# An attention and window-convolution kernel: x channels spread over 128 partitions, three of every four used

## The chip, the cores and the metric

The kernel runs on one core of one Trainium2 chip. The metric is the device time of one execution in microseconds; the time before is the median of three runs, 3556.07 us (3543.9 to 3556.36).

## The reference

One image of 48 channels and 256 x 256 pixels goes through two layers, each with a group normalisation ahead of it and a residual around it.

```python
# layer 0: x (1, 48, 256, 256), 16 groups of 3 channels in _gn
qkv = einsum('bchw,oc->bohw', _gn(x), w_qkv)        # 144 channels
q, k, v = split(dwconv3x3(qkv, w_dw), 3)            # depthwise 3x3
q, k, v = heads(unfold(.))                          # 4x4 patches, 8 heads, 96 x 4356
attn = softmax(_l2norm(q)^T _l2norm(k) * temperature)
x = x + einsum('bchw,oc->bohw', fold(v attn^T), w_proj)
# layer 1: windows of 64 x 64
x = x + sum_t einsum('bcphqw,wW,hH,cC->bCpHqW', windows(_gn(x)), Ws[t], Hs[t], Cs[t])
```

The patches of the outer border are all zero; they count only in the softmax's sum.

## The kernel before

All is float32. Channels lie on partitions. Image tensors with 48 channels are held as two halves: upper image rows (or the upper of two parts of a tile) on partitions 16 to 63, lower ones on 64 to 111; partitions 0 to 15 are cleared (`OFF = 16`, `PF = 112`, `rows_of`). `begin` moves one such tensor with two transfers of 48 rows, one for each half, in turn on the queues it is given.

The work goes through these stages.

1. **Head.** x is loaded into `xr` in ten parts (`parts`, most of 16 image rows of each half) over the queues of SyncE and ScalarE, while ScalarE clears the first 16 partitions (`clear`, L120). VectorE takes statistics of each two image rows as a part is there (`bn_stats`, L451), then `group_stats` makes mean and 1/deviation of each group with two products with `gm`. They are folded into the weights: `wq` (two heads) and `wr` (six heads), both held twice, for the two halves, and into `bias`. `gm`, `wq`, `wr` and `wp` (the projection) are zeroed by VectorE and filled by small loads on the GpSimd queue (L98 to L114), `wq` and `wr` copied from half to half by a transfer (L112).
2. **First convolution.** The product with `wq` for two heads (L512), out of `xr`, with ScalarE and VectorE in turn adding the bias into `oi` (L521, L523), and stores to the DRAM tensor `t1[0]`, 36 channels in transfers of 32 and 4 (L528), half of them on SyncE, half on GpSimd.
3. **Depthwise convolution of head 0** (`depthwise_first`), whose outcome goes to DRAM (`qkv`) in patch order.
4. **Attention**, head by head in an order written out by hand: `scores` (L370, L638), `weigh` (L672), and between them the depthwise convolution of the next head, and, in head 0, the product for the other six heads strip by strip (`Strip`, `xs`, L203). In the last head the first three x tiles of the projection (`xt`) and most of the first patch tile (`pot0`, in `kt` buffers) are loaded on SyncE.
5. **Projection** (`project`, L837), eight tiles in `order`: the product with `wp` over patches (`pot`, loaded on SyncE from `os_`, L907), the residual added in place by VectorE (L844), statistics (L846), and a store to the DRAM tensor `x1s` on GpSimd. x tiles from the fourth on (`pxt`, `pieces`) are loaded on SyncE and ScalarE. `pieces` (`lxq`) stays and is the first band of the last layer.
6. **Last layer**: over channels (L1008, weights `csn`, which also carry the mean through a partition that holds ones), over w (L1032), over h (L1051), the residual (L1065), the output on GpSimd (L1069). Loads of the next rows and pieces are issued one at a time on SyncE (`begin_load`), each behind a tiny transfer (`turns`) that waits for work just done; `load_piece` is one transfer of 48 rows and four image rows.

Stages 1, 2 and 5 are put in order by the framework's scheduler within each engine, except TensorE's order in parts of 5; stages 4 and 6 are in the order as written. A hardware transfer of SyncE or ScalarE uses one of eight semaphores in turn, and so waits for the one eight before it.

Of the kernel before, what the change touches and what calls it, by code (L numbers as in the profile page):

```python
# [21 lines left out]
OFF = 16  # L22
PF = OFF + P2
# [26 lines left out]
def conv_preact_kernel(  # L50
# [44 lines left out]
    rows_of = [slice(OFF + s * C, OFF + (s + 1) * C) for s in range(2)]  # L95
    gm = const.tile([PF, PF], F32, name="gm")
    nc.vector.memset(gm, 0.0)
    nc.gpsimd.dma_start(out=gm[OFF:, OFF:], in_=gmat)  # L98
    wq = const.tile([PF, 64], F32, name="wq")
    nc.vector.memset(wq, 0.0)  # L100
    wr = const.tile([PF, M1], F32, name="wr")
    nc.vector.memset(wr, 0.0)
    wp = const.tile([PF, PF], F32, name="wp")
    nc.vector.memset(wp, 0.0)
    for h in range(NH):
        o = h * HC if h < H0 else (h - H0) * HC
        nc.gpsimd.dma_start(
            out=(wq if h < H0 else wr)[rows_of[0], o : o + HC].rearrange("c (z e) -> c z e", z=3),
            in_=w_qkvT.rearrange("c (z h e) -> h c z e", z=3, h=NH)[h],
        )  # L110
    for w in (wq, wr):
        nc.gpsimd.dma_start(out=w[rows_of[1]], in_=w[rows_of[0]])  # L112
    for r in rows_of:
        nc.gpsimd.dma_start(out=wp[r, r], in_=w_projT)  # L114

    def clear(t, n=OFF, value=0):

        _, a, b = t.shape
        to = plain[:n, value : value + 1].rearrange("p (u v) -> p u v", u=1).to_broadcast([n, a, b])
        nc.scalar.copy(t[:n], to)  # L120
# [7 lines left out]
    taps = ExitStack()  # L128
    diag = taps.enter_context(tc.tile_pool(name="diag", bufs=1)).tile([NP1, 9, NP1], F32, name="diag")
# [43 lines left out]
    def begin(to, rows, engs, into=True):  # L173

        for s in range(2):
            a, b = (to[rows_of[s]], rows[s])
            engs[s % len(engs)].dma_start(out=a if into else b, in_=b if into else a)
# [9 lines left out]
    class Strip:  # L187
# [5 lines left out]
        def load(self):  # L193
            self.xs = xss[self.j % len(xss)]
            begin(self.xs, both_halves(xc, SR * self.j, SR), (nc.sync,))

        def run(self, pool):
            self.ot = ots[self.j % len(ots)]
            for i in range(0, SR, 2):
                ps = pool.tile([128, 2, 512], F32, name="big")  # L200
                for s in range(2):
                    r = slice(s * 64, min(PF, s * 64 + 64))
                    nc.tensor.matmul(  # L203
                        ps[:M1, s, :],
                        lhsT=wr[r],
                        rhs=self.xs[r, i : i + 2, :].rearrange("p a b -> p (a b)"),
                        start=True,
                        stop=True,
                    )
# [223 lines left out]
    with tc.tile_pool(name="xn", bufs=1) as xnp, tc.tile_pool(name="cst", bufs=1) as cst, tc.tile_pool(  # L433
# [10 lines left out]
        parts = [16] * 7 + [8, 4, 4]  # L444
        st0 = cst.tile([PF, HALF * W // 512, 6], F32, name="st0")
        for i, LR in enumerate(parts):
            j = sum(parts[:i])
            begin(xr[:, j : j + LR, :], both_halves(xc, j, LR), (nc.sync, nc.scalar))
            clear(xr[:, j : j + LR, :])
            for i in range(0, LR, 2):  # L450
                nc.vector.bn_stats(st0[:, (j + i) // 2, :], xr[:, j + i : j + i + 2, :].rearrange("p a b -> p (a b)"))  # L451
        group_stats(st0, mean0, rstd0, cst, nps)
        for g, w in enumerate((wq, wr)):
            nc.vector.tensor_scalar_mul(w, w, rstd0)
            m = w.shape[1]
            pb = nps.tile([128, 1], F32, name="pb0", tag="pstat")
            if g:
                nc.tensor.matmul(pb[:m], lhsT=w[:64], rhs=mean0[:64], start=True, stop=True)
# [45 lines left out]
        for n in range(QR // OR):  # L504
            ot = ois[n % len(ois)]
            for i in range(0, OR, 2):
                ps = pw.tile([128, 2, 512], F32, name="pw")
                for c in range(2):
                    for s in range(2):
                        r = slice(s * 64, min(PF, s * 64 + 64))  # L510
# [13 lines left out]
            for c in range(2):  # L524
                to = t1[0][:, 1 : H + 1, :].rearrange("c (s y) x -> c s y x", s=2)
                to = to[:, :, c * QR + n * OR : c * QR + (n + 1) * OR, :]
                for a, b in ((0, 32), (32, M0)):
                    (nc.gpsimd if c else nc.sync).dma_start(out=to[a:b], in_=ot[c * 64 + a : c * 64 + b])  # L528
# [10 lines left out]
    xss = [cv.tile([PF, SR, W], F32, name=f"xs{i}") for i in range(2)]  # L539

    def edges():
# [4 lines left out]
        for t in xss:  # L546
            nc.gpsimd.memset(t[:OFF], 0.0)

# [39 lines left out]
    with tc.tile_pool(name="ahead", bufs=2) as ah, tc.tile_pool(name="ae", bufs=3) as ae, tc.tile_pool(  # L588
# [113 lines left out]
        def load_pot0(ki, half, c0, c1, eng):  # L702
# [3 lines left out]
            r = OFF + half * C  # L706
# [14 lines left out]
        with tc.manual_schedule():  # L721
# [3 lines left out]
            for h in range(NH):  # L725
                more = h + 1 < NH
                rows = {r: Depthwise(h + 1, r) for r in range(CR + 1)} if more else {}
                for g in range(NG):
                    p, d, n = rows.get(g - 2), rows.get(g - 1), rows.get(g)

                    if not more and g == 0:
# [4 lines left out]
                        for t in xts:  # L736
                            nc.gpsimd.memset(t[:OFF], 0.0)
                        pot0 = [ah.tile([128, 2, 512], F32R, name="kt", bufs=14) for _ in range(KS)]
                        pot0 = [t.bitcast(F32).rearrange("p a (b n) -> p (a b) n", b=2) for t in pot0]
                        for t in pot0:  # L740
                            nc.gpsimd.memset(t[:OFF], 0.0)
# [87 lines left out]
        def project(k, pot, part, xt, new):  # L829
# [4 lines left out]
            for ki in range(KS):  # L834
                ps = new(PY)
                for y in range(0, PY, 2):
# [3 lines left out]
                        rhs=pot(ki)[:PF, :, (part * PY + y) * PX : (part * PY + y + 2) * PX],  # L840
# [9 lines left out]
        def in_big(n):  # L850

            ps = big.tile([128, 2, 512], F32, name="big")
            return ps[:PF].rearrange("p a (b x) -> p (a b) x", x=W)
# [21 lines left out]
    def load_piece(yw, i, s, y, n, eng):  # L875

        y0 = yw * WS + s * HW + i * PR + y
        eng.dma_start(out=piece(yw, i)[rows_of[s], y : y + n, :], in_=x1s[:, y0 : y0 + n, :])

    with tc.tile_pool(name="pjx", bufs=1) as pjx, tc.tile_pool(name="pj", bufs=1) as pj, tc.tile_pool(name="pjs", bufs=1) as pjs, tc.tile_pool(  # L880
# [4 lines left out]
        pots = [pj.tile([PF, KK, NP], F32, name=f"pot{t}") for t in range(3)]  # L885
        for t in pots + pxts:
            clear(t)
        clear(pieces.rearrange("p a y x -> p (a y) x"), 64 + CF, 1)
        csn = l1c.tile([64 + CF, T3 * C], F32, name="csn")
        nc.gpsimd.memset(csn, 0.0)  # L890
        for r in rows_of:
            nc.scalar.dma_start(out=csn[r].rearrange("c (t d) -> c t d", t=T3), in_=Cs.rearrange("t c d -> c t d"))
        at = pjs.tile([PF, PF + 1], F32, name="at")
        nc.gpsimd.memset(at, 0.0)
        for o in (0, PF):
            nc.gpsimd.memset(at[:, o : o + 1], 1.0)

        def both_pieces(i):

            return pieces[:PF, i : i + 2].rearrange("p a y x -> p (a y) x")  # L900

        xus = [[xts[1]], [xts[2]], [pxts[0]], [pxts[1]], [pieces[:PF, NPC], pxts[2]], [both_pieces(2)]]
        xus.append([pieces[:PF, 0], pieces[:PF, 1]])
        for k, xus_k in enumerate(xus, 1):
            yw, i = order[k]
            ot = pots[k % 3]
            nc.sync.dma_start(out=ot[OFF:], in_=ov[yw * 2 + i])  # L907
# [22 lines left out]
        with tc.manual_schedule(engines={mybir.EngineType.PE}):  # L930
# [5 lines left out]
            mcol = pjs.tile([PF, PF + 1], F32, name="mcol")  # L936
            nc.vector.tensor_scalar_mul(mcol, at, mean1)
            occupy(nmx)
            nc.vector.tensor_scalar_mul(csn[:PF], csn[:PF], rstd1)
# [202 lines left out]
```

## Time and profile before

| | |
|---|---|
| median of three runs | 3556.07 us |
| profiled execution, its own time | 3557.27 us |
| its span, first to last instruction | 3555.5 us |
| mean granted TensorE clock | 0.979 |
| TensorE matmul busy | 3314.1 us (93%) |
| VectorE busy | 1958.1 us (55%) |
| ScalarE busy | 1952.7 us (55%) |
| GpSimd busy | 589.7 us (17%) |
| moved by DMA | 380.20 MB, mean 107 GB/s |

A busy share is an average over stages that differ. The page's 40 slices of 89 us show the busy tenths of each engine, the tenths of the 16 DMA engines and the GB/s that they moved. The view by stage gives for a window the busy time of each engine with the number of its instructions, the granted clock, the DMA share and GB/s. The waits name who waited for whom, with the total, the number and the longest. The chain of waits follows the work that ended last back from step to step.

### The profile page before, as it was taken

How to read it: one execution, taken by the hardware profiler on the slowest of the kernel's cores; microseconds unless marked ns; L12 is line 12 of the kernel's file. 1: busy time of each engine (PE TensorE's matmuls, PEld its weight loads, DVE VectorE, ACT ScalarE, POOL GpSimd, SP SyncE). 2: the span in 40 equal slices, each digit the busy share in tenths (PEclk: the TensorE clock that was granted, in tenths of full speed). 3: DMA queues.
4: the chain of work that ended last, by engine and by line, in shares of the span. 5: the costliest groups of instructions: out<-in, count | busy, mean ns of one | idle time of the engine just before them, and what ended most of it. 6: DMA issues, size and time to landing. Idle time of an engine off the chain costs nothing.

```text
span 3555.5 us, 63466 instructions
## 1 busy us (share of the span) xinstructions
PE 3314.1 (93%) x25964; PEld 1852.0 (52%) x25964; DVE 1958.1 (55%) x2965; ACT 1952.7 (55%) x2891; POOL 589.7 (17%) x660
## 2 busy tenths in 40 slices
PE   0596999999999999999999999999999999996898
PEld 0243455555555555555555555555555555542576
DVE  5272666138834882588258825882687222226544
ACT  3234676657755765566556655765576444442243
POOL 2221111012211221122012201220122020000123
PEclk9898999999999999999999999999999999997999
DMA  8546666543332333233333333333233322119764
GB/s 146 139 126 156 162 167 159 165 139 95 87 87 76 93 87 86 79 95 85 83 91 96 81 86 86 95 80 88 83 93 88 79 65 49 30 38 257 205 165 113
DMA packets 232498, 380.20 MB, mean 107 GB/s; under 512 B 77794, under 2 KB 176482, under 8 KB 229128
## 3 DMA queue, kind: packets, MB, share of 16 engines
q1 hardware_dynamic: 191094, 252.76, 26.1%
q0 software_dynamic: 36544, 110.12, 13.9%
q10 hardware_dynamic: 4562, 13.19, 1.9%
q8 instruction: 207, 3.39, 0.4%
q14 instruction: 91, 0.75, 0.1%
HBM read 230.82 MB, written 144.90 MB: 106 GB/s over the span
## 4 chain that ended last, share of the span: by engine, by line
PE 86%; DMA 5%; DVE 2%; SPq 1%; ACT 1%; issue 1%; ACTq 0%; POOL 0%; POOLq 0%; DVEq 0%
PE big L370 39%; PE big L672 36%; PE pb L1032 2%; PE pa L1008 2%; DMA xs<-in_x_dram 2%; PE pc L1051 2%; DMA pot<-os__70 2%; PE big L203 2%; PE dps L247 1%; DVE acc L258 1%; PE pst L615 1%; SPq L344 0%; DVE st L846 0%; DMA kt<-qkv 0%; DMA pad<-t 0%
## 5 line engine op out<-in xcount | busy, mean ns | idle before, releaser
L638 ACT ACTIVATE e<-big,nmx 128x1024 f32<-128x1024 f32 x1024 | 1144.1, 1117 | 899.8 <-PE big L370 887.3
L370 PE MATMUL big<-kt,qt 128*128 128x512 f32 x6144 | 1458.2, 395 | 26.8 <-DMA kt<-qkv 24.5
L672 PE MATMUL big<-e,vn 128*32 128x512 f32 x12288 | 1348.5, 593 | 1.0 <-DVE vn L656 1.0
L370 PEld LDWEIGHTS big<-kt,qt 128*128 128x128 f32 x6144 | 1142.4, 189 | 367.1 <-issue 120.2
L686 DVE TENSOR_TENSOR oacc<-big,oacc 128x1024 f32<-128x1024 f32 x359 | 438.4, 1221 | 768.2 <-PE big L672 768.2
L672 PEld LDWEIGHTS big<-e,vn 128*32 128x32 f32 x12288 | 384.5, 110 | 881.9 <-issue 815.8
L258 DVE SCALAR_TENSOR_TENSOR acc<-pad,dwt,acc 126x1024 f32<-126x1024 f32 x592 | 765.5, 1293 | 34.4 <-ACT acc L239 18.7
L328 POOL DMA_DIRECT2D qkv<-o x72 | 52.8, 734 | 1336.6 <-ACT o L312 1336.6
L322 POOL TENSOR_TENSOR ol<-o,oh 126x1024 fp32r<-126x1024 f32 x78 | 185.2, 2374 | 273.2 <-DVE ss L273 198.0
L652 DVE TENSOR_REDUCE zt<-zs 128x1 f32<-128x5 f32 x256 | 38.6, 151 | 325.1 <-ACT e L638 288.6
L638 ACT ACTIVATION_READ_ACCUMULATOR e<-big,nmx 128x1 f32 x1024 | 195.9, 191 | 0.0
L312 ACT COPY o<-acc 126x1024 f32<-126x1024 f32 x74 | 161.5, 2183 | 0.0
L239 ACT ACTIVATE acc<-pad,dwt 126x1024 f32<-126x1024 f32 x74 | 84.1, 1136 | 86.0 <-DMA pad<-t 76.7
L210 ACT ACTIVATE ot<-big,bias 108x1024 f32<-108x1024 f32 x64 | 68.1, 1111 | 113.4 <-PE big L203 76.1
L1039 ACT COPY lyt<-pb 128x1024 f32<-128x1024 f32 x69 | 69.8, 1012 | 107.0 <-PE pb L1032 107.0
L697 POOL DMA_DIRECT2D os__70<-oacc x86 | 50.3, 593 | 424.1 <-DVE oacc L686 414.3
L247 PE MATMUL dps<-pad,diag 126*126 126x512 f32 x216 | 96.5, 607 | 22.9 <-DMA pad<-t 22.9
L269 ACT ACTIVATE sq<-acc 126x1024 f32<-126x1024 f32 x74 | 78.2, 1057 | 59.6 <-DVE acc L258 48.5
L344 POOL DMA_DIRECT2D kt<-qkv x44 | 22.9, 542 | 518.8 <-PE big L370 507.7
L273 DVE TENSOR_REDUCE ss<-sq 126x64 f32<-126x1024 f32 x80 | 97.3, 1218 | 6.5 <-ACT sq L269 6.5
L1018 DVE COPY lzt<-pa 128x864 f32<-128x864 f32 (+1 forms) x69 | 67.3, 998 | 59.6 <-PE pa L1008 59.6
L837 PE MATMUL pps<-pot,wp 112*112 112x512 f32 x112 | 60.9, 699 | 39.5 <-DVE pxt L844 22.6
(154 smaller groups left out, 1944.3 us busy)
## 6 DMA issues: line engine op xcount, KB each, us to landing
pad<-t SPq DMA_DIRECT2D x238, 254.0 KB
t<-ot SPq DMA_DIRECT2D x64, 435.4 KB
qkv<-ol POOLq DMA_DIRECT2D x78, 336.0 KB, 6.5
qkv<-oh POOLq DMA_DIRECT2D x70, 336.0 KB, 5.9
qt<-qkv SPq DMA_DIRECT2D x176, 96.0 KB
xs<-in_x_dram SPq DMA_DIRECT2D x64, 192.0 KB
out_dram<-lrt POOLq DMA_DIRECT2D x96, 128.0 KB, 3.6
qkv<-o POOLq DMA_DIRECT2D x72, 168.0 KB, 3.5
```

The costliest lines, as they stand in the source:

```text
L203: nc.tensor.matmul(ps[:M1, s, :], lhsT=wr[r], rhs=self.xs[r, i : i + 2, :].rearrange("p a b -> p (a b)"), start=True, stop=True,)
L239: nc.scalar.mul(self.acc, self.pad[:, 0:KS, 0:W], dwt[:, self.h, 0:1])
L247: nc.tensor.matmul(ps[:, i, :], lhsT=diag[:, tap, :], rhs=self.pad[:, y : y + 2, dx : dx + W], start=(tap == 0), stop=(tap == 8),)
L258: nc.vector.scalar_tensor_tensor(self.acc, self.pad[:, dy : dy + KS, dx : dx + W], dwt[:, self.h, tap : tap + 1], self.acc, ALU.mult, ALU.add,
L269: nc.scalar.activation(self.sq, self.acc, AF.Square)
L273: nc.vector.tensor_reduce(self.ss, self.sq.rearrange("p a (x b) -> p x a b", b=KS), AX.XY, ALU.add)
L312: nc.scalar.copy(self.o.rearrange("p (a b) x -> p a b x", a=KS), self.acc.rearrange("p a (x b) -> p a b x", b=KS))
L322: eng.tensor_sub(self.ol, self.o, self.oh.bitcast(F32))
L370: nc.tensor.matmul(ps[:, i, :], lhsT=qt[:, r, q0 : q0 + 128], rhs=kts[2 * j + i][:, r // 2, :], start=(r == 0), stop=(r == 2),)
L638: nc.scalar.activation(e[:, j * 1024 : (j + 1) * 1024], ps.rearrange("p a b -> p (a b)"), AF.Exp, bias=nmx[:, b : b + 1], accum_out=zs[:, ...
L672: nc.tensor.matmul(ps[p * 32 : (p + 1) * 32, u, :], lhsT=vn[:, c * 32 : (c + 1) * 32], rhs=e[:, n * 512 : (n + 1) * 512], start=(i == 0), ...
L686: nc.vector.tensor_add(oaccs[h, pair], ps, old)
```

## The change

The halves now lie on partitions 0 to 63 and 64 to 127, and in each group of four partitions three hold channels and the fourth a fill (`SP3 = 4`, `PF = 128`). `begin` and `load_piece` move a half with three transfers of 16 rows at steps of four partitions (every third channel each). The fill is written to all 128 partitions of the tile ahead of the load, with 0 in the head and 1 from the projection on, so that the fourth partitions serve as the ones of the last layer.

Weights come into this layout on the chip: each is loaded once, densely, with 48 channels on 48 partitions, and TensorE multiplies it with a matrix of ones and zeros (`spread`, `one_half`, `twice`). `xs` and `wr` keep 48 dense partitions a half, at 0 and 64; the statistics are brought there by products with `fold`. `pot` has 96 dense partitions from 0 on, and `wp` maps these to the 128. x is loaded in eight parts of other sizes, and the statistics are written after all loads in the program. The stores of the first convolution are one transfer of 36 rows instead of 32 and 4.

```diff
-OFF = 16
-PF = OFF + P2
+SP3 = 4
+PF = 128
-    rows_of = [slice(OFF + s * C, OFF + (s + 1) * C) for s in range(2)]
+    rows_of = [[slice(s * 64 + k, (s + 1) * 64, SP3) for k in range(3)] for s in range(2)]
-    nc.gpsimd.dma_start(out=gm[OFF:, OFF:], in_=gmat)
-    for h in range(NH):
-        o = h * HC if h < H0 else (h - H0) * HC
-        nc.gpsimd.dma_start(out=(wq if h < H0 else wr)[rows_of[0], o : o + HC]...)
-    for w in (wq, wr):
-        nc.gpsimd.dma_start(out=w[rows_of[1]], in_=w[rows_of[0]])
-    for r in rows_of:
-        nc.gpsimd.dma_start(out=wp[r, r], in_=w_projT)
-    def clear(t, n=OFF, value=0):
...
+        nc.gpsimd.dma_start(out=w48, in_=w_qkvT)
+        nc.gpsimd.dma_start(out=g48, in_=gmat[0:C, 0:C])
+        nc.gpsimd.dma_start(out=p48, in_=w_projT)
...
+        ps = through(spread, w48)
+        nc.vector.tensor_copy(mixed(wq, H0), by_head(ps, 0, H0))
+        ps = through(twice, w48)
+        nc.vector.tensor_copy(mixed(wr, NH - H0), by_head(ps, H0, NH))
+        nc.vector.tensor_copy(fold, through(one_half[:, 0], twice))
+        nc.vector.tensor_copy(gs, through(g48, spread))
+        nc.vector.tensor_copy(gm, through(spread, gs))
...
+        nc.vector.tensor_copy(wp, through(wt[:, 0], one_half[:, 0], [(wt[:, 1], one_half[:, 1])]))
+    def fill(t, eng, value=0.0):
+        if eng is nc.scalar:
+            _, a, b = t.shape
+            src = plain[:, int(value) : int(value) + 1].rearrange("p (u v) -> p u v", u=1)
+            eng.copy(t, src.to_broadcast([128, a, b]))
+        else:
+            eng.memset(t, value)
     def begin(to, rows, engs, into=True):
-        for s in range(2):
-            a, b = (to[rows_of[s]], rows[s])
-            engs[s % len(engs)].dma_start(out=a if into else b, in_=b if into else a)
+        for k in range(3):
+            for s in range(2):
+                a, b = (to[rows_of[s][k]], rows[s][k::3])
+                engs[s % len(engs)].dma_start(out=a if into else b, in_=b if into else a)
...
-            begin(self.xs, both_halves(xc, SR * self.j, SR), (nc.sync,))
+            for s, rows in enumerate(both_halves(xc, SR * self.j, SR)):
+                nc.sync.dma_start(out=self.xs[s * 64 : s * 64 + C], in_=rows)
...
-        parts = [16] * 7 + [8, 4, 4]
+        parts = [8, 24, 32, 32, 16, 8, 4, 4]
         for i, LR in enumerate(parts):
             j = sum(parts[:i])
+            fill(xr[:, j : j + LR, :], nc.vector if i in (0, 2) else nc.scalar)
             begin(xr[:, j : j + LR, :], both_halves(xc, j, LR), (nc.sync, nc.scalar))
-            clear(xr[:, j : j + LR, :])
-            for i in range(0, LR, 2):
+        for j in range(0, HALF, 16):
+            for i in range(0, 16, 2):
                 nc.vector.bn_stats(...)
...
+                nc.tensor.matmul(pf[:, 0:1], lhsT=fold, rhs=mean0, start=True, stop=True)
+                nc.tensor.matmul(pf[:, 1:2], lhsT=fold, rhs=rstd0, start=True, stop=True)
...
-                for a, b in ((0, 32), (32, M0)):
-                    (nc.gpsimd if c else nc.sync).dma_start(out=to[a:b], in_=ot[c * 64 + a : c * 64 + b])
+                (nc.gpsimd if c else nc.sync).dma_start(out=to, in_=ot[c * 64 : c * 64 + M0])
...
                         for t in xts:
-                            nc.gpsimd.memset(t[:OFF], 0.0)
+                            nc.gpsimd.memset(t, 1.0)
-                        for t in pot0:
-                            nc.gpsimd.memset(t[:OFF], 0.0)
...
-        eng.dma_start(out=piece(yw, i)[rows_of[s], y : y + n, :], in_=x1s[:, y0 : y0 + n, :])
+        for k in range(3):
+            eng.dma_start(out=piece(yw, i)[rows_of[s][k], y : y + n, :], in_=x1s[k::3, y0 : y0 + n, :])
...
-        for t in pots + pxts:
-            clear(t)
-        clear(pieces.rearrange("p a y x -> p (a y) x"), 64 + CF, 1)
+        pots = [pj.tile([P2, KK, NP], F32, name=f"pot{t}") for t in range(3)]
+        fill(pxts[0], nc.scalar, 1.0)
+        fill(pxts[1], nc.scalar, 1.0)
+        fill(pieces.rearrange("p a y x -> p (a y) x"), nc.scalar, 1.0)
+        fill(pxts[2], nc.scalar, 1.0)
+        nc.scalar.dma_start(out=c48.rearrange("c (t d) -> c t d", t=T3), in_=Cs.rearrange("t c d -> c t d"))
+        nc.tensor.matmul(pcs, lhsT=spread, rhs=c48, start=True, stop=True)
+        nc.vector.tensor_copy(csn, pcs)
...
-            nc.sync.dma_start(out=ot[OFF:], in_=ov[yw * 2 + i])
+            nc.sync.dma_start(out=ot, in_=ov[yw * 2 + i])
```

## The prediction

> **What bounds the kernel now.** I read the page's 40 slices first, then the table by stage (busy time of each engine in chosen windows), then the chain of waits, and for the two stages that the change touches the waits and the timeline.
>
> The slices and the page's chain:
>
> ```profile
> PE   0596999999999999999999999999999999996898
> DMA  8546666543332333233333333333233322119764
> GB/s 146 139 126 156 162 167 159 165 139 95 87 87 76 93 87 86 79 95 85 83 91 96 81 86 86 95 80 88 83 93 88 79 65 49 30 38 257 205 165 113
> ...
> PE 86%; DMA 5%; DVE 2%; SPq 1%; ACT 1%; issue 1%; ACTq 0%; POOL 0%; POOLq 0%; DVEq 0%
> ```
>
> TensorE is full for some 30 slices in the middle (the attention, 753 to 3160 us). Nothing of the change lies on that path. It is idle at the start and thins out near the end, exactly where the DMA row is high. So the change is worth what it does at the two ends. The stages there:
>
> ```profile
> 14.00:24.00 10.00, 0.00 (x0) 0.00 (x0) 6.58 (x22) 3.47 (x2) 1.14 (x2) 1.00 1.02 161
> 24.00:34.00 10.00, 0.00 (x0) 0.00 (x0) 4.95 (x9) 3.38 (x1) 1.20 (x3) 1.00 1.06 173
> ...
> 110.00:116.00 6.00, 5.84 (x56) 2.03 (x48) 3.74 (x3) 2.39 (x3) 3.32 (x6) 1.00 0.92 234
> ...
> 3230.00:3256.00 26.00, 4.59 (x11) 1.59 (x9) 5.97 (x10) 0.00 (x0) 1.02 (x2) 0.63 1.02 265
> 3256.00:3285.00 29.00, 21.73 (x37) 8.19 (x38) 28.07 (x40) 1.28 (x1) 4.10 (x8) 0.79 1.02 243
> 3285.00:3302.00 17.00, 10.97 (x18) 3.81 (x17) 7.46 (x10) 0.00 (x0) 1.02 (x2) 0.80 1.00 311
> ```
>
> The columns are window, length, busy us of PE, PEld, DVE, ACT, POOL, the clock, the DMA share and GB/s. While x is loaded (0.7 to 75 us) the 16 DMA engines are busy all the time, yet move only 160 to 173 GB/s. In the projection (3197 to 3302) they are full too, at 243 to 311. The stores of the first convolution reach 234 GB/s with 0.92 of the engines. So a full DMA queue can go faster than it does on x.
>
> Who waits for it, at the start and in the projection (from the waits and the chain):
>
> ```profile
> DVE st L451 <- DMA xr<-in_x_dram: 29.2, 5, 12.1
> ...
> L451 DVE BATCH_NORM_STATS2 st<-xr 112x6 f32<-112x512 f32 x64 | 38.6, 676 | 30.5 <-DMA xr<-in_x_dram 29.2 <-issue 1.3
> ...
> 3229.47 26.14 DMA pot<-os__70
> ...
> 3268.26 32.87 DMA pot<-os__70
> ```
>
> VectorE's statistics are 38.6 us of work drawn out to 84.4 us. In the projection two stretches of 26 and 33 us are waits for loads (the chain names pot; VectorE was waiting for the x piece, which landed behind it).
>
> **The change, part by part.**
>
> *Loading x (head).* The group's data must land before statistics can end. Work on the parts is released by their landing at 13.65, 23.52, 33.42, 42.64 and 51.78 us, 9.5 us per 16 rows (1.57 MB, both halves), 165 GB/s; all 12.58 MB take 73.5 us. Each transfer of 48 rows becomes three of 16 rows.
>
> The trace has no such transfer. The nearest row is the store of the first convolution, 234 GB/s, which would give 53.8 us. [...] I take 57.5 us.
>
> [...] x's channels lie 256 KiB apart, before and after. If that holds x at 165 GB/s, nothing is gained. The stores at 234 GB/s have a pitch that is no power of two, so the trace doesn't exclude it. This is a rival below.
>
> *Fills.* A load now waits for a fill of its rows on all 128 partitions; before, 16 rows were cleared beside the load. VectorE: `row` 1x1134 took 1.00 us, 0.88 ns an element, so 1.8 us (8 image rows) and 7.2 us (32). ScalarE: 128x10240 took 8.72 us, so 5.2 us for 24 rows, 7.0 for 32, 3.6 for 16. In the program's order the first fill stands eleventh on VectorE, at about 1.9 us: the first transfers start at 3.8 us instead of 0.7, the second part at 7.7 (table load to 2.5, then 5.2 us); the first part's 0.79 MB cover 3.6 us of that. Later fills (14 us of ScalarE) stand behind at most eight transfers in flight, 1.9 MB or more of a queue's own, some 17 us. Cost: 3 us, in the sum. If the cover were gone, 7 us more.
>
> *Weights through products.* Three loads replace thirteen (`gm`, `wq`, `wr`, `wp`) on POOL's queue. The old ones crawled behind x (`wr` landed after 37.6 us); the new ones are issued by about 4 us, when x has hardly begun. Eight products and about 12 small VectorE copies (0.15 to 0.3 us each, 0.5 us for a product as in `pm`) now stand ahead of the statistics on VectorE: it ends fills at about 11.5 us and this chain at about 20 us. The first 32 image rows land at 19.4, so it costs about 1 us. If `p48` landed as late as `wr` did, statistics would start at 40 us and end at 79.
>
> *Statistics.* 64 x 0.604 us. Landing at 0.45 us per image row from 5 us on: parts at 20.4 (32 rows), 34.8, 49.2, 56.4, 60, 62, 63.5. VectorE: 20.5 to 30.2, 34.8 to 44.5, 49.2 to 58.9, then in one run to 63.7, 66.1, 67.3, 68.5. Before: 84.4. **Head: -16 us.** Behind it two `fold` products stand on TensorE before the second convolution product: +1 us.
>
> *First convolution.* One store of 36 rows for two of 32 and 4. Engines move at 1.71 us a step, stalls for stores were 19.8 us on ScalarE in seven waits, covered in part by catching up later. Bytes are the same. From -5 (fewer landings to wait for) to +5: taken as 0. POOL issues half as many, and its 21 `dwt` loads end soon after x does, ahead of its first store.
>
> *Attention.* `xs` keeps 48-row transfers, at 0 and 64 instead of 16 and 64; the chain's 1.8% of waits for it stays. The matmuls have the same columns, so the same time. In the last head each piece of `xt` takes six issues for two: 4 x 0.4 = 1.6 us more of SyncE per 11 us; cover: SyncE waits 1153 us in total for TensorE, and queries are loaded two groups ahead. POOL's three fills have the same 4096 elements. 0 us; without cover, 2 us a piece, 20 us.
>
> *Projection.* The bytes are eight tiles out (12.6 MB), seven `pot` (11.0), five x (7.9). Loads and stores up to 3301 are about 29 MB in 105 us, 277 GB/s. [...] First, SyncE now issues the `pot` of tile 2 ahead of the last four small `kt` loads instead of behind them: 1.57 MB, 5.7 us of a full queue, start about 4 us earlier, while `kt` lands up to as much later; ScalarE's four `kt` loads run beside it. Second, x into `pxt` waits for a fill, 3.6 us behind tile 0's products; the queue has `pot` and stores to move meanwhile. [...] 29 MB then take 97 us from 3192: end at 3289 for 3301. **-13 us** (bounds: +4 at an unchanged rate with the fills in the way, -21 at 330). POOL issues 40 more transfers at 0.51 us, 20 us in 100, with 12 of 130 busy. `c48` and its product cost 0.5 us where TensorE waited for VectorE anyway.
>
> *Last layer.* 88 more piece loads at about 0.4 us are 35 us of SyncE, which waits 82 us there for `lyt` and `lzt`: 0 us.
>
> **Sum.** The profiled execution took 3557.3 us (span 3555.5), 1.2 above the median of the runs, 3556.1. -16 + 1 + 0 + 0 - 13 + 0 = -28: 3529 against the profile, **3528** against the median.
>
> **The rivals.**
> 1. [...] For: pitch unchanged, 165 GB/s with all engines busy. [...] x ends at 5 + 73.5 = 78.5, statistics at 81.5: -3 + 1. Projection: only the earlier `pot`, -4. 3550. Chance 0.22.
> 2. [...] Chance 0.20.
> 3. *Slower: eight in flight.* In the program's order each transfer of SyncE and ScalarE waits for the one eight before it. A turn of the last layer with a piece is now four transfers, so two turns are in flight. Turns come about every 2.5 us; from a landing time of 5 us on, SyncE falls behind and TensorE waits for pieces. Landing there: 3.6 us for the output (POOL), share 0.6 to 0.7. At 6 us each of 44 turns is 0.7 to 1 us late: +30 to +44 in that layer, with the gains of rival 1 about 3585. For: bursts at share 0.9. Against: pieces are asked for a band ahead. Chance 0.13.
>
> The step of the sum stands at 0.45. Its own range is 3514 to 3538.
>
> **How the numbers follow.** A measurement of this kernel can tell about 0.5% (18 us) from no change. Faster by more than that: the step of the sum and rival 2, 0.65. Within: rival 1, 0.22. Slower: rival 3, 0.13. Low end 3500 (rival 2 with a shorter convolution stage), high end 3566 (rival 1 with 15 us of covers gone); about 0.05 lies below and 0.14 above.
>
> **What would show it.** Right: a first x transfer near 4 us, x moving at about 220 GB/s, BATCH_NORM_STATS2 ending near 68, the first convolution from about 83; projection at about 300 GB/s without the waits of 26 and 33 us; the middle unchanged. Wrong: still 165 GB/s on x (rival 1); statistics starting after 25 us (the weights are late); SyncE waiting for landings in the last layer, longer than 230 us (rival 3).

## The result: 0.14% faster, not 0.8%, and the profile after

| | before | after |
|---|---|---|
| median | 3555.3 us (20 runs, 3543.0 to 3569.8) | 3548.6 us (20 runs, 3539.1 to 3557.3) |
| ratio, 95% interval | | 0.9986 (0.9975 to 0.9997) |
| span of the profiled execution | 3555.5 us | 3546.9 us |
| mean granted clock | 0.979 | 0.977 |

Forecast were 3528 us, 28 less. Some 5 (by the ratio) to 7 (by the medians) came. The page after, the slices and the chain:

```profile
PE   2678999999999999999999999999999999987798
DMA  6555666533332332333233323332333212129554
GB/s 146 179 116 160 173 168 165 169 110 93 80 86 84 94 91 77 86 96 93 77 87 96 88 79 86 95 88 78 85 94 91 77 45 54 26 72 305 136 148 114
...
PE 86%; DMA 5%; DVE 2%; SPq 1%; ACT 1%; issue 1%; ACTq 0%; POOL 0%; POOLq 0%; DVEq 0%
```

TensorE is at work earlier (the first two slices hold 2 and 6 tenths, before 0 and 5), and the slice of the projection moves 305 GB/s for 257. The third slice from the end is the surprise: it begins where the projection is over, and TensorE has 7 tenths there, less than the 8 of before. The table by stage (columns as before) for x and for the projection:

```profile
14.00:24.00 10.00, 3.94 (x14) 2.26 (x12) 6.17 (x26) 4.00 (x1) 1.69 (x3) 1.00 1.04 231
24.00:34.00 10.00, 0.00 (x0) 0.00 (x0) 7.08 (x12) 6.52 (x2) 1.13 (x2) 1.00 1.05 227
...
3190.00:3220.00 30.00, 24.51 (x49) 10.26 (x49) 27.17 (x36) 17.53 (x4) 8.18 (x17) 0.88 1.00 306
3220.00:3245.00 25.00, 20.43 (x35) 7.53 (x34) 23.73 (x35) 0.00 (x0) 7.25 (x15) 0.81 1.01 357
```

The DMA engines were full before as well; now the same full share carries 231 and 227 GB/s for 161 and 173, and up to 357 in the projection. In the group of the statistics the wait for x fell from 29.2 to 12.8 us. In the chain of waits the two stretches of 26 and 33 us in the projection gave way to three shorter ones:

```profile
L501 DVE BATCH_NORM_STATS2 st<-xr 128x6 f32<-128x512 f32 x64 | 38.4, 677 | 12.8 <-DMA xr<-in_x_dram 12.8
```
```profile
3203.92 16.36 DMA pxt<-in_x_dram
3220.29 14.71 DMA lxq<-in_x_dram
...
3241.29 23.69 DMA pot<-os__70
```

A stretch of the chain runs from a load's issue to its landing, and the three together are hardly less than the two before (55 us for 59). What shrank is the idle time at their ends. VectorE's longest wait for a load before,

```profile
DVE pxt L844 <- DMA pot<-os__70: 20.0, 1, 20.0
```

has become one of 8.5 us, and TensorE's waits in the projection sum to 35 us for 49.

So the two ends of the change did what they were to do. The gain was given back behind them. The following table splits each profiled execution: until the end of x's statistics; from the first product of the first convolution to the first depthwise product; from there to the start of the last group of attention products (88 matmuls); from that to the end of the projection's statistics; from the first product of the last layer to the end. The ratio (and interval) is that of all runs to the kernel before on the same chip. The lower rows are the experiments below.

| kernel | statistics end | first conv. | attention | projection | last layer | ratio |
|---|---|---|---|---|---|---|
| before | 84.4 | 80.1 | 3010.4 | 134.4 | **235.3** | 1 |
| after | 70.4 | 71.1 | 3010.2 | 121.7 | **261.9** | 0.9986 (0.9975-0.9997) |
| e1: after, pieces of 8 rows | 69.6 | 73.4 | 3005.0 | 118.6 | 239.7 | 0.9908 (0.9888-0.9928) |
| e2: after, one issue a piece | 70.2 | 74.5 | 3006.5 | 120.3 | 233.4 | 0.9921 (0.9896-0.9946) |
| e3: after, three `lyt` | 70.2 | 72.8 | 3007.0 | 118.6 | 245.3 | 0.9941 (0.9922-0.9959) |
| e4: before, piece split in 3 | 79.0 | 80.1 | 3002.2 | 132.9 | 241.4 | 1.0011 (0.9998-1.0023) |
| e5: after, x in 3 x 16 neighbours | 101.2 | 75.5 | 3002.9 | 116.1 | 255.3 | 1.0084 (1.0051-1.0117) |
| e6: after, x in one of 48 | 87.1 | 76.8 | 3016.4 | 118.4 | 258.3 | 1.0051 (1.0034-1.0069) |
| e7: after, stores 32 + 4 | 70.5 | 79.0 | 3007.1 | 118.5 | 256.5 | 1.0006 (0.9991-1.0020) |
| e8: after, projection in one of 48 | 67.5 | 73.3 | 3009.6 | 132.2 | 257.1 | 1.0030 (1.0020-1.0040) |
| e9: before, stores of 36 | 75.5 | 74.2 | 2995.4 | 130.4 | 239.4 | 0.9985 (0.9965-1.0004) |
| e10: after, 8 rows, three `lyt` | 68.9 | 75.1 | 3010.7 | 117.6 | 233.9 | 0.9921 (0.9898-0.9944) |
| e11: after, piece in 3 x 16 neighbours | 70.3 | 73.6 | 3012.1 | 118.2 | 238.8 | 0.9949 (0.9929-0.9969) |
| e12: before, pieces of 8 rows | 76.6 | 79.4 | 3006.9 | 132.9 | 251.3 | 1.0021 (1.0005-1.0036) |

From before to after: -14.0, -9.0, 0, -12.7 and **+26.6**. Three quarters of all that was won is lost in the last layer. (The attention is the same code with the same work in all rows and scatters by 20 us from one execution to the next, so stages are compared with stages here, and totals only by ratios.)

**The last layer, read.** Its waits, before and then after (engine and line waited for what: total, times, longest):

```profile
ACT lyt L1039 <- PE pb L1032: 107.0, 62, 2.9
...
PE pb L1032 <- ACT lyt L1039: 1.4, 2, 1.1
```
```profile
ACT lyt L1093 <- DMA turns<-lyt: 33.1, 4, 12.8
...
PE pb L1086 <- ACT lyt L1093: 23.4, 7, 10.0
```

Two lines grew out of nothing. TensorE waits 23.4 us for ScalarE to empty its PSUM tile into `lyt`, and ScalarE cannot write, because a turn's tiny transfer (`turns`) that must still read the old contents of this `lyt` buffer has not been made. It stands in SyncE's program, and SyncE is late: in the longest wait (3331.59 to 3344.34 us) the turn's transfer that ends it is issued at 3342.83 and has landed 1.4 us later. SyncE's own waits in that layer (`SPq` is its queue of instructions), before and after:

```profile
SPq L993 <- ACT lyt L1039: 53.8, 22, 13.9
SPq L993 <- DVE lzt L1018: 28.1, 15, 9.5
```
```profile
SPq L1047 <- ACT lyt L1093: 16.0, 7, 14.0
SPq L1047 <- DVE lzt L1072: 9.6, 3, 6.8
...
SPq L929 <- DMA lrt<-x1s: 1.0, 2, 0.7
```

Of the 82 us that SyncE had to spare 26 are left, and a piece load (L929) waits for a landing only 1.0 us in all (all its waits for landings in the layer sum to 8.5 us; before it was 8.9). Its timeline shows where the 56 us went; a burst before, and the same burst after:

```profile
3347.99 0.31 SPq L878 DMA_DIRECT2D lxq<-x1s  x1
3348.39 0.22 SPq L993 DMA_DIRECT2D turns<-lzt  x1
3349.43 0.31 SPq L878 DMA_DIRECT2D lxq<-x1s  x1
3349.83 0.22 SPq L993 DMA_DIRECT2D turns<-lzt  x1
```
```profile
3338.69 1.75 SPq L929 DMA_DIRECT2D lxq<-x1s  x3
3340.53 0.37 SPq L1047 DMA_DIRECT2D turns<-lzt  x1
3341.00 1.73 SPq L929 DMA_DIRECT2D lxq<-x1s  x3
3342.83 0.37 SPq L1047 DMA_DIRECT2D turns<-lyt  x1
```

Before, a turn is 0.31 + 0.22 us, with gaps in which SyncE waits for work (3348.61 to 3349.43). After, the three issues take 1.73 to 1.75 us (0.47 the first, 0.58 each of the others, 0.05 between them) and the turn's transfer 0.37, with no gap that is a wait in these lines. In seven of the twelve turns counted next they take longer, up to 3.03 us, since single issues last up to 1.86 us. Such an issue was not waiting for the transfer eight before it, which had landed by then; why it is long stays open. From the first to the thirteenth piece load of this burst the starts run from 3345.74 to 3359.72 us before (1.17 us a turn) and from 3309.84 to 3343.30 after (2.79 us a turn). TensorE's work asks for a turn every 1.2 us just there; SyncE makes one in 2.8.

### The profile page after: what moved, and what is told of

Its sections match the earlier page's. It is cut to its first block, busy times and chain, and to the rows that moved or that the text cites. A ratio compares the mean times of both kernels' runs of the same rounds, so it can differ in the third digit from the quotient of the medians.

```text
span 3546.9 us, 63775 instructions
## 1 busy us (share of the span) xinstructions
PE 3323.5 (94%) x25985; PEld 1860.2 (52%) x25985; DVE 1973.0 (56%) x2984; ACT 1933.1 (55%) x2884; POOL 589.1 (17%) x667
## 4 chain that ended last, share of the span: by engine, by line
PE 86%; DMA 5%; DVE 2%; SPq 1%; ACT 1%; issue 1%; ACTq 0%; POOL 0%; POOLq 0%; DVEq 0%
PE big L419 39%; PE big L724 37%; PE pb L1086 2%; PE pa L1062 2%; PE pc L1105 2%; PE big L252 2%; DMA xs<-in_x_dram 1%; PE dps L296 1%; DMA pot<-os__70 1%; DVE acc L307 1%; DMA pxt<-in_x_dram 1%; SPq L929 1%; PE pst L667 1%; DMA lxq<-in_x_dram 0%; PE pn L326 0%
## 5 line engine op out<-in xcount | busy, mean ns | idle before, releaser
L307 DVE SCALAR_TENSOR_TENSOR acc<-pad,dwt,acc 126x1024 f32<-126x1024 f32 x592 | 765.4, 1293 | 33.1 <-ACT acc L288 17.3
L288 ACT ACTIVATE acc<-pad,dwt 126x1024 f32<-126x1024 f32 x74 | 84.0, 1135 | 77.9 <-DMA pad<-t 68.5
L1086 PE MATMUL pb<-wsb,lzt 64*64 64x64 f32 x4608 | 86.4, 225 | 30.1 <-ACT lyt L1093 23.4
L1086 PEld LDWEIGHTS pb<-wsb,lzt 64*64 64x64 f32 x4608 | 79.5, 139 | 50.2 <-ACT lyt L1093 24.8
```

The lines of the kernel that those rows point to most:

```text
L288: nc.scalar.mul(self.acc, self.pad[:, 0:KS, 0:W], dwt[:, self.h, 0:1])
L307: nc.vector.scalar_tensor_tensor(self.acc, self.pad[:, dy : dy + KS, dx : dx + W], dwt[:, self.h, tap : tap + 1], self.acc, ALU.mult, ALU.add,
L1086: nc.tensor.matmul(pb[s * WS : (s + 1) * WS, w, n * WS : (n + 1) * WS], lhsT=zts[u][r, t * C + b * 24 + q * 8 + s * 4 + i, :], rhs=wsb[r, ...
```

## The experiments

Theory: the last layer lost its time to SyncE's issuing of piece loads, felt through the buffers of `lyt`. Rival: the landing times of the pieces with eight transfers in flight (the third rival of the prediction). Beside these, each gain is undone alone. "Ports" in the expectations is the author's name for a limit that depends on the partitions on which a transfer's rows lie; no run shows a port.

**e1: pieces of eight rows.** One `load_piece` of `PR` rows instead of two of `PR // 2`:

```diff
-                    for y in range(0, PR, PR // 2):
-                        loads.append(lambda s=s, y=y: load_piece(yw, i, s, y, PR // 2, nc.sync))
+                    loads.append(lambda s=s: load_piece(yw, i, s, 0, PR, nc.sync))
```

> The changed kernel, with the pieces of the last layer loaded eight image rows at a time instead of twice four: two turns with three piece issues for each piece instead of four. Theory (SyncE's issues): the last layer takes 262 us instead of 235 because a turn with a piece keeps SyncE busy for 2.3 to 3 us (three issues of 0.58 us and a turn's transfer of 0.37, one behind the other), while TensorE needs one turn about every 2.5 us; SyncE falls behind, and ScalarE waits for the turn's transfer that still has to read `lyt` (33.1 us in four waits). With 22 such turns instead of 44 it saves about 50 us of SyncE: the waits of `lyt` for `turns` go to under 8 us, the layer to 235 to 242 us, the time to 3522 to 3530. Rival (landing times with eight in flight): a turn with a piece is still four transfers, and each moves twice the bytes and lands later; half the turns are late by more: about half of the 26 us comes back, 3535 to 3541, and SyncE shows waits for landings of `lxq`. Rival (the loss has nothing to do with piece loads, but with the 128-row pieces that TensorE reads): 3548.

The layer took 239.7 us, and the ratio was 0.9908: 33 us less than before (26 to 40). Of the two lines of the waits only a trace is left; ScalarE's wait for `turns` is not among its waits any more:

```profile
PE pb L1085 <- ACT lyt L1092: 1.8, 4, 1.1
```

With twice the bytes in each piece load and still four transfers to such a turn, the landing rival would have kept half of the loss. SyncE's issues in the layer sum to 88.6 us here, to 149.3 after the change and to 68.4 before it.

**e2: one issue of 48 rows for each piece.**

```diff
-        for k in range(3):
-            eng.dma_start(out=piece(yw, i)[rows_of[s][k], y : y + n, :], in_=x1s[k::3, y0 : y0 + n, :])
+        eng.dma_start(out=piece(yw, i)[s * 64 : s * 64 + C, y : y + n, :], in_=x1s[:, y0 : y0 + n, :])
```

> The changed kernel, with each piece of four image rows loaded by one transfer of 48 neighbouring rows (partitions 0 to 47 or 64 to 111) instead of three of 16 at steps of four; the channels of these pieces so lie on other partitions than the weights assume. SyncE's issues: as before the change, one issue and one turn's transfer each: the layer back to 235 us, the time to 3520 to 3527. If it is the data (ports, landing) and not the number of issues, 48 rows on neighbouring partitions land no earlier: 3540 to 3549. The issue itself: 0.31 us if it is the 48 rows or the neighbouring partitions that make it short, as in the kernel before.

233.4 us, as short as before the change, and the issue is back at 0.31 us:

```profile
3312.30 0.31 SPq L928 DMA_DIRECT2D lxq<-x1s  x1
3312.70 0.22 SPq L1046 DMA_DIRECT2D turns<-lzt  x1
```

Everything else of the change is in this kernel, and its ratio, 0.9921, is -28 us (-37 to -19): what the prediction's sum gives where the last layer costs nothing.

**e3: a third `lyt` buffer** (`tc.tile_pool(name="ly", bufs=3)`), all issues as they are.

> The changed kernel with three `lyt` buffers instead of two; all issues as they are. If TensorE loses its time because ScalarE can't write `lyt` before a late turn's transfer has read it, a third buffer gives SyncE another 19 us to catch up, which is more than the longest wait of 12.8 us: the waits of `lyt` for `turns` go, and the layer falls to 235 to 245 us, the time to 3522 to 3533, with SyncE as busy as ever. If the pieces themselves come too late, TensorE waits for them (`pa` <- `lxq`) instead, and the time stays at 3543 to 3549.

245.3 us: 16.6 of the 26.6 us came back, so the path does lead through `lyt`. But the waits did not go, as was expected; they shrank:

```profile
ACT lyt L1093 <- DMA turns<-lyt: 22.0, 4, 11.0
...
PE pb L1086 <- ACT lyt L1093: 12.0, 6, 8.0
```

One more buffer covers part of the lateness of a burst, not all of it. TensorE still waits for `lyt` and not for pieces.

**e4: the kernel before, with three issues of 16 neighbouring rows for each piece.**

```diff
-        eng.dma_start(out=piece(yw, i)[rows_of[s], y : y + n, :], in_=x1s[:, y0 : y0 + n, :])
+        for k in range(0, C, 16):
+            r = slice(OFF + s * C + k, OFF + s * C + k + 16)
+            eng.dma_start(out=piece(yw, i)[r, y : y + n, :], in_=x1s[k : k + 16, y0 : y0 + n, :])
```

> The kernel before, with each piece load of 48 rows split into three of 16 neighbouring rows; nothing else changes, and no step of four. If the number of issues is the cause, the last layer grows from 235 to about 260 us and the time to 3576 to 3586; the three issues take about 0.58 us each, as after the change. If the steps of four make the issue long, they take 0.31 us each: then a turn takes about 1.5 us, and the layer stays below 243 us, 3555 to 3563. If the loss came from something else of the change, 3555.

This told against the plain form of the theory: three issues alone cost next to nothing (1.0011, the layer 241.4 us). SyncE's timeline says why:

```profile
3347.42 0.22 SPq L995 DMA_DIRECT2D turns<-lzt  x1
3347.74 1.23 SPq L880 DMA_DIRECT2D lxq<-x1s  x3
3349.07 0.22 SPq L995 DMA_DIRECT2D turns<-lyt  x1
```

Of three issues of 16 neighbouring rows the first takes 0.30 us, as one of 48 does (0.31), and each of the others 0.41; at steps of four it was 0.47 and 0.58. The turn's transfer behind them takes 0.22, not 0.37. The expectation had 0.58 or 0.31 for each. From turn to turn that is 1.65 us here for the 2.3 of three issues at steps of four without a pause.

**e11: the changed kernel, three issues of 16 neighbouring rows**, which asks the same from the other side, and is the sharpest test of the landing rival: as many transfers, as many bytes.

```diff
-        for k in range(3):
-            eng.dma_start(out=piece(yw, i)[rows_of[s][k], y : y + n, :], in_=x1s[k::3, y0 : y0 + n, :])
+        for k in range(0, C, 16):
+            r = slice(s * 64 + k, s * 64 + k + 16)
+            eng.dma_start(out=piece(yw, i)[r, y : y + n, :], in_=x1s[k : k + 16, y0 : y0 + n, :])
```

> The changed kernel, with each piece of four image rows loaded by three transfers of 16 neighbouring rows instead of three at steps of four (the channels of these pieces so lie on other partitions than the weights assume). The number of transfers and their bytes stay; x in the head was slower in this form than in any other. If the landing of the pieces is what makes SyncE late, the layer is 262 us or longer, the ratio 0.998 to 1.003. If it is SyncE's time to issue, then 0.41 us an issue and 0.22 a turn's transfer, as the split in the kernel before had, against 0.58 and 0.37: the layer 239 to 245 us, the ratio 0.991 to 0.9945.

238.8 us, ratio 0.9949 (the layer just below what was expected, the ratio just above). From issue to landing a piece load takes 2.8 us here and 2.8 after the change (medians of the 132 loads, by the updates of their semaphores; 4.2 before), and still all but 3.5 of the 26.6 us are gone. Landing is out; what is left is the time of the issues themselves, which sum to 120.1 us of SyncE for 149.3. This run takes neighbouring partitions and neighbouring channels, where the changed kernel takes every fourth partition and every third channel; which of the two makes an issue longer is not shown.

**e10: eight rows and three buffers together** (the edits of e1 and e3).

> The changed kernel with pieces loaded eight image rows at a time and three `lyt` buffers. Eight rows alone gave a last layer of 239.7 us, three buffers alone 245.3, one issue a turn 233.4. Theory (SyncE's issues, felt through `lyt`): what eight rows leave of lateness the third buffer covers; the layer 233 to 237 us, the ratio to the kernel before 0.988 to 0.991. If both only move the same wait to the pieces, 239 to 241 us and 0.990 to 0.992.

The layer is the shortest with steps of four, 233.9 us; the total, 0.9921, just above both ranges, is not distinguishable from e1's.

**e12: the kernel before with pieces of eight rows** (the edit of e1).

> The kernel before, with the pieces of the last layer loaded eight image rows at a time; nothing else. If eight rows only take SyncE's issues off the path that the change put there, nothing is gained here, where SyncE waits 82 us of the layer for work: the layer 233 to 240 us, the ratio to the kernel before 0.999 to 1.001. If larger pieces are a gain of their own (fewer waits, a faster queue), the layer falls below 230 us and the ratio below 0.998; then not all of the 0.9% of the changed kernel with such pieces is the change's.

Expected was no difference, and it is 0.2% slower, the layer 251.3 us. So larger pieces are no gain of their own. Why they cost here is not settled. Part of the time is in waits without a releaser, 4.8 us in eight before; the matmuls of the layer take 6.5 us more, at a granted clock of 0.96 for 0.99:

```profile
PE pb L1031 <- issue: 12.3, 11, 3.9
```

TensorE's ten waits of this kind over 0.5 us (two of them ahead of `pa`) all end 2.3 to 3.1 us after the start of a 16 KiB packet on the queue of instructions (q8 of the page, one packet in some 5 us). So they look like waits for instructions; no run tests it, nor why they are longer here.

**e5 and e6: x in the head by neighbouring rows**, in three transfers of 16 (e5, shown), and in one of 48, `xr[s * 64 : s * 64 + C, ...]` (e6); fills and parts as after.

```diff
-            begin(xr[:, j : j + LR, :], both_halves(xc, j, LR), (nc.sync, nc.scalar))
+            for k in range(0, C, 16):
+                for s, rows in enumerate(both_halves(xc, j, LR)):
+                    eng = (nc.sync, nc.scalar)[s]
+                    eng.dma_start(out=xr[s * 64 + k : s * 64 + k + 16, j : j + LR, :], in_=rows[k : k + 16])
```

> The changed kernel, with x in the head loaded by three transfers of 16 neighbouring rows a half (partitions 0 to 15, 16 to 31, 32 to 47, and 64 on) instead of three at steps of four; x's channels so lie on other partitions than the weights assume. Fills, parts and number of transfers stay. Theory (ports): what counts is how the rows lie, not how many transfers there are; x moves at about 165 GB/s again, the statistics end at 82 to 86 us instead of 70.4, the time is 3559 to 3565. Rival (smaller or more transfers keep the 16 DMA engines better fed): 218 to 231 GB/s, 70 us, 3548.

> The changed kernel, with x in the head loaded by one transfer of 48 neighbouring rows a half, as before the change, at partitions 0 and 64; the channels so lie on other partitions than the weights assume. Ports: 165 GB/s, statistics end at 82 to 86 us, time 3559 to 3565, like the run with three neighbouring transfers. More transfers: 165 GB/s here, but not there. The pitch of x in HBM or the parts of other sizes as the limit: as fast as after the change, 3548.

Both slower: statistics end at 101.2 and 87.1 us, e5 far beyond the 82 to 86 expected, e6 just beyond. The table by stage, e5 and then e6:

```profile
24.00:34.00 10.00, 0.00 (x0) 0.00 (x0) 0.00 (x0) 5.90 (x1) 1.13 (x2) 1.00 1.05 187
44.00:54.00 10.00, 0.00 (x0) 0.00 (x0) 0.00 (x0) 0.00 (x0) 0.57 (x1) 1.00 0.96 108
```
```profile
24.00:34.00 10.00, 0.00 (x0) 0.00 (x0) 6.40 (x11) 2.84 (x2) 0.74 (x2) 1.00 1.00 158
44.00:54.00 10.00, 0.00 (x0) 0.00 (x0) 5.98 (x11) 1.04 (x1) 0.62 (x2) 1.00 1.02 167
```

With the same x and the same number of transfers, the choice of rows divides 231 GB/s (after) from 90 to 187 (e5). But it has two sides. The changed kernel also takes every third channel, 768 KiB apart in HBM, where e5 and e6 take neighbouring channels, 256 KiB apart. No run has one without the other. That a pitch of 256 KiB does not hold x at 165 GB/s is shown by e9 and e12, whose loads in the form of before reached 220 and 212. Whether the partitions or the pitch make e5 and e6 slow stays open.

**e7 and e9: the stores of the first convolution**, 32 + 4 rows in the changed kernel, 36 in the kernel before.

```diff
-                (nc.gpsimd if c else nc.sync).dma_start(out=to, in_=ot[c * 64 : c * 64 + M0])
+                for a, b in ((0, 32), (32, M0)):
+                    (nc.gpsimd if c else nc.sync).dma_start(out=to[a:b], in_=ot[c * 64 + a : c * 64 + b])
```

> The changed kernel, with the stores of the first convolution in two transfers of 32 and 4 rows again instead of one of 36. The stage from the first product of the first convolution to the first depthwise product took 80.1 us before and 71.1 after. If the two stores are the reason (twice the transfers, eight at a time in flight, so ScalarE and VectorE wait for buffers), the stage is 78 to 82 us again and the time 3555 to 3559. If the reason lies elsewhere (bytes in x's place, GpSimd's queue free earlier), the stage stays at 71 to 73 us and the time at 3548 to 3550.

> The kernel before, with the stores of the first convolution as one transfer of 36 rows instead of 32 and 4; nothing else. With the change undone in this one place the stage (first product of the first convolution to first depthwise product) went from 71.1 to 79.0 us. If this edit alone is worth it, the stage is 71 to 73 us here instead of 80.1 and the ratio to the kernel before 0.9973 to 0.9982. If it pays only where x's load has left the queues free earlier, the stage stays at 78 to 80 us and the ratio at 0.999 to 1.001.

The stage is 79.0 us with two stores in the changed kernel and 74.2 with one in the kernel before: in both directions it goes with the store, not with the layout (e9 stays above the 71 to 73 expected). ScalarE's waits for stores to land, e7 first and e9 second; the longest is 7.0 us with two stores (7.7 in the kernel before) and 4.9 with one (4.3 after the change):

```profile
ACT oi L579 <- DMA t<-oi: 23.2, 9, 7.0
```
```profile
ACT oi L523 <- DMA t<-oi: 18.6, 6, 4.9
```

The sums of these waits differ less than their longest (19.8 us before, 18.4 after); TensorE's waits for ScalarE's `oi` are 14.7 us before and 13.9 in e7, 10.6 after and 10.2 in e9. As totals e7's 1.0006 (0.9991 to 1.0020) and e9's 0.9985 (0.9965 to 1.0004) cannot be told from the kernel before.

**e8: the projection by transfers of 48 neighbouring rows**, loads and stores (`begin48` for `begin` on `xt`, `pxt` and `pieces`).

```diff
+    def begin48(to, rows, engs, into=True):
+        for s in range(2):
+            a, b = (to[s * 64 : s * 64 + C], rows[s])
+            engs[s % len(engs)].dma_start(out=a if into else b, in_=b if into else a)
...
-                    begin(xt, both_parts(xc, k, part * R, R), (nc.sync, nc.scalar))
+                    begin48(xt, both_parts(xc, k, part * R, R), (nc.sync, nc.scalar))
```

> The changed kernel, with the projection's x tiles loaded and its results stored by one transfer of 48 neighbouring rows a half instead of three of 16 at steps of four; the channels so lie on other partitions than the weights assume. The head and the last layer stay. Projection, from the last attention product to the end of its statistics: 134.4 us before, 121.7 after. If balanced ports made the gain, 130 to 135 us and 3557 to 3562; if the patch tile issued earlier and the other order of loads made it, 121 to 124 us and 3548 to 3551; fewer issues on GpSimd and SyncE can give up to 3 us back in either case.

132.2 us, 10.5 more than after. TensorE's waits in the projection are 46 us again, for 35 after, and the long stretches of the chain are back:

```profile
3200.05 31.21 DMA pxt<-in_x_dram
3231.33 31.32 DMA pot<-os__70
```

So the form of the transfers made this gain, and the `pot` issued earlier is worth little by itself. Partitions, channels and the number of transfers change together here; that the number is not what counts is shown for the head alone (e5).

## Why the prediction was wrong, by its own steps

**The step that failed** is the shortest one: "88 more piece loads at about 0.4 us are 35 us of SyncE, which waits 82 us there for `lyt` and `lzt`: 0 us." It measured +26.6 us in the profiled pair, and about +20 as a mean of the rows (257.8 us over after, e5, e6, e7 and e8, against 237.4 over before and e9). Three terms of it were wrong.

- *Price.* An issue of 16 rows at steps of four takes 0.58 us, and the old one took 0.31; the turn's transfer behind it takes 0.37 for 0.22. A turn with a piece goes from 0.53 to 2.11 us of bare issuing (0.09 to 0.10 us lie between issues besides): 1.58 more, times 44 turns, is 70 us, not 35. In the trace SyncE's issues in the layer sum to 149.3 us for 68.4, 81 more, as 23 of the 132 piece issues took 0.7 us or longer (e4 and e11 have 21 and 19 of these). SyncE's spare time fell by 56; the rest came out as a longer layer.
- *Cover.* 82 us is a sum over the layer. The pieces come in bursts of some 16 turns, and in a burst there is no such slack: the timeline of before has a turn each 1.17 us there. At 2.79 us a turn SyncE is 19 us late after the 12 turns counted above.
- *What is late next.* The prediction asked only whether pieces would be late. First came the `lyt` buffer, which the late turn's transfer had still to read.

About a fifth of the loss is not waiting but slower matmuls, at a lower granted clock. In the first burst and behind it the table by stage has

```profile
3305.00:3325.00 20.00, 19.01 (x582) 15.19 (x584) 8.12 (x8) 7.71 (x9) 2.57 (x4) 1.00 0.60 146
3325.00:3345.00 20.00, 10.16 (x280) 7.79 (x278) 5.44 (x6) 4.80 (x5) 5.01 (x8) 0.85 0.49 129
3345.00:3365.00 20.00, 14.71 (x342) 12.40 (x344) 4.55 (x5) 5.75 (x7) 2.50 (x4) 0.76 0.66 161
```

TensorE is busy 10 of 20 us, and the granted clock falls to 0.85 and 0.76. Its matmuls take 219.8 us in the layer for 214.6 before, 5.3 more, beside 22.0 more of waiting for `lyt`; that makes the 26.6, within a microsecond. That the waits lower the clock is the author's reading of these rows; no run tests it by itself.

**The third rival** had the place, and its size of 30 to 44 us was near, but not its mechanism. SyncE was to wait for landings; its piece loads waited 1.0 us for them, and e1 and e11, with as many transfers in flight for each turn, took the loss away. It was given 0.13. The landing was the wrong resource to count; the time to issue, 149.3 us of SyncE for 68.4, was the right one.

**Right, with sizes.**
- *Loading x:* predicted about 220 GB/s and statistics until 68.5 us; 207 to 231, and 70.4 (69.7 in the mean of the eight kernels with this head). First transfers at 4.09 us (predicted 3.8), statistics from 19.2 (20.5). No run shows where the 57.5 us taken for all of x come from; in the profile after, its transfers ran from 4.09 until the last landed at 65.3, 61.2 us. Rival 1's 165 GB/s fell; for rival 2, which stands behind the low end of 3500, 3548.6 us are far too long. That the spread over the partitions is the reason is not shown: "x's channels lie 256 KiB apart, before and after" is true of the tensor, but each of the new transfers takes every third channel, which the prediction did not count. But the head before is not always at 84.4: it ended at 79.0, 75.5 and 76.6 in e4, e9 and e12, with windows of up to 220 GB/s. By the packets of the two queues, in stretches of 2 us between 24 and 40 us, e12 moves 90 to 131 GB/s on each at the same time, while before one of the two falls to 16 to 57 in five stretches of eight. So the 9.5 us per 16 rows that the prediction read in the trace of before are not a fixed price of that form. On average the head gained 9 us, not 14 to 16.
- *First convolution:* taken as 0, from -5 to +5; the profile had -9. The means (73.4 us over the seven kernels with the new head, dense or not in the projection, and one store; 79.7 over the four with two stores) have -6. The step had the reason (fewer landings to wait for) and bounded it at -5.
- *Attention:* 0 predicted; 3010.4 and 3010.2. A matmul out of `xs` took 589 ns (median) before and after, on 48 and 64 partitions before and 48 after.
- *Projection:* -13 predicted, -12.7 measured. No run shows where the 300 GB/s behind its 97 us and the 330 of its bounds come from; three stretches after moved 306, 357 and 266 GB/s. That the spread over the partitions made it is not separated from the channels (e8). And the two stretches of 26 and 33 us were not waits all through: TensorE was busy for 21.7 of the 29 us from 3256 on, and VectorE's waits in them are 20.0 and 8.8 us.
- *Slips of the working,* each too small to matter: x moved at 156 to 173 GB/s before, not 160 to 173; the first 32 rows land at 19.4 us in one place and at 20.4 in another; 3289 for 3301 is -12, not -13; and a first convolution "from about 83" does not follow from its sum, which gives 75 (89.7 before; it was 76.3).

By the means the steps ahead of the last layer come to about -9, -6 and -14, the prediction had -15, 0 and -13: two errors that cancel, by luck. Its sum of -28 is what e2 measured, where the last layer costs nothing.

## What to carry to other kernels

Where a change cuts a transfer into several, price the issues on the queue's engine by the timeline, in the burst, against the pace that the work there asks for; the engine's idle time over the stage (82 us here) did not tell that 26.6 would be lost. Look up what that engine's late instructions read: here markers that had still to read `lyt` held up its next writer for 33.1 us. And try a bulk load with its rows spread over the partitions and channels, as here for x (207 to 231 GB/s for 156 to 173) and the projection (121.7 us for 134.4), but keep transfers that are issued in bursts few: here twice the rows in each piece (e1) turned 0.14% into 0.9%.

## What the runs showed of the hardware

- The time to issue a transfer from SyncE depends on its pattern: 0.31 us for one of 48 neighbouring rows (before, e2); of three of 16 neighbouring rows 0.30 for the first and 0.41 for each of the others (e4, e11), of three at steps of four 0.47 and 0.58 (after). The tiny transfer behind it changes too, 0.22 us or 0.37. In the forms with three issues 19 to 23 of 132 took 0.7 us or longer, up to 1.86 (after, e4, e11).
- A full DMA share is no rate: the same x moved at 90 to 187 (e5), 144 to 187 (e6) and 207 to 231 GB/s (after) with a DMA share of 0.92 to 1.25 (0.79 where e5 moved 90), by the rows and channels that a transfer takes. The form of before alone moved it at 143 to 220 in four executions.
- Beside TensorE's longer waits its matmuls were slower: with 22 us more of waiting in the last layer, 10.0 us the longest, they took 5.3 us more, at a granted clock of 0.94 for 0.99 (after). In e3, with 12.0 us of such waits and none over 8.0, it was 0.4 us more, at 0.98.
